# Moving GpSimd combinations, a small matmul and two activations to other places in a two-layer graph-network kernel

One core of one Trainium2 chip. The metric is the device time of one execution, in microseconds (us), as the median of several executions. All executions of this study were in the fast state. Where two kernels are compared by a ratio, it is the mean time of one kernel's fast runs over that of the other's of the same rounds, so it is not quite the ratio of the medians that are quoted beside it. "Slower than after" or "faster than after" by so many us is the difference of two medians. The runs were timed in several rounds, in which the kernel before had medians from 3920.30 to 3922.25 us; a difference of a few us is therefore also read from the traces.

## What is computed

32 graphs of 512 nodes with 512 features, one adjacency matrix for all. Two layers, both with a residual, all in float32:

```python
# layer 0
h = relu(layernorm(x))
q, k, v = h @ Wq + bq, h @ Wk + bk, h @ Wv + bv          # 8 heads of 64
attn = softmax(q @ k.T / 8 + (1 - adj) * -1e9)
x = x + (attn @ v) @ Wo + bo
# layer 1
h = relu(layernorm(x))
g = h @ W                                                # 512 x 512
e = leaky_relu(g @ a1 [:, None] + g @ a2 [None, :], 0.2) * adj
x = x + elu(softmax(e) @ g + beta * g)
```

## The kernel before

The kernel works on three graphs at once. In step b of its loop, layer 0 of graph b (V and four head pairs) runs beside the last projection (Wo) of graph b-1, layer 1 of graph b-2, and the transposes, K and Q of graph b+1. Every projection (V, K, Q, Wo) is done in blocks with seven products instead of eight; a product is 16 matmuls and takes TensorE 1.73 us. The right-hand blocks of these products are differences of blocks, "combinations", which GpSimd makes: three in `combos`, the fourth in `fourth`.

```python
def combos(b, name, pairs):                 # three GpSimd operations
    ...
    nc.gpsimd.tensor_tensor(t3, b22, b12, op=ALU.subtract)
    nc.gpsimd.tensor_tensor(b12, b12, b11, op=ALU.subtract)
    nc.gpsimd.tensor_tensor(t2, b22, b12, op=ALU.subtract)

def turn(b, st):                            # part N: transposes of graph b
    ...
    nc.scalar.activation(h[0], p, AF.Relu)
    st["hT"] = combos(b, "tT", h)           # for V, K and Q of that graph

def values(b, j, st):                       # head pair j, once its exponentials are there
    need("rd"); need("e"); need("es")
    po = st["po"] = psum.tile([P, N], F32, ..., tag="po")
    ...                                     # po = attention times v, 16 matmuls
    pd = st["pd"] = psum.tile([P, N], F32, ..., tag="pd")
    ...                                     # pd = column sums of the exponentials, 4 matmuls

def finish(b, j, st):                       # reciprocal of pd on VectorE, then o * rd on GpSimd
    for k in range(2):
        later("rd", 0.0, GAP[(j + 1) % NP] - 4.0, 1.7, lambda k=k: divide(k))

def unit(b, j):
    values(...)                             # of the pair before
    for k, tag in enumerate(("s", "xy", "qz", "s")):
        scores(b, j, k, s, tag)             # four score products of this pair
    finish(...)                             # of the pair before

order = {
    0: "0V1N2c3wKQ", 1: "0VU1r2NRW3KQ", B - 1: "0VDU1G2rYRW3", B: "0DUGrRWY", B + 1: "DGY",
}.get(b, "0VDU1G2rYNRW3KQ")
```

The string at the end is the order of the parts in a step: digits are the units of head pairs; D, G and Y are layer 1 (row sums `pe` and diagonal, the gather `pg`, the product `py`); U makes Wo's combinations; r and R add the residual; W is Wo. `later`, `then` and `need` do not run anything on the chip. They decide at build time, with a small model of the clock, where in VectorE's, ScalarE's and GpSimd's instruction streams an operation is written: `later` puts it where the model sees room, `need` writes at once all that is outstanding of a kind. GpSimd took its operations in the written order here: where the change below writes the three combinations behind Wo's own, GpSimd's timeline has them behind too (L348 at 2575.07 us after L356 at 2571.37; before, L348 at 1047.24 ahead of L356 at 1054.50). The names in the profile: `y_w`, `qz_w` are accumulators of Wo's products, `_k` of K's; `ps` scores, `po` attention output, `pd` denominators, `pe` layer 1's row sums. A bank is one accumulator of TensorE's output memory; `pd` has one, so a new pd waits until VectorE has read the last one (29 waits of up to 2.0 us for the reciprocals `rd` in the kernel before).

Of the kernel before, what the change touches and what calls it, by code (L numbers as in the profile page):

```python
# [20 lines left out]
P = 128  # L21
# [40 lines left out]
def kernel(  # L62
# [122 lines left out]
        now = max(clock["dve"], clock["pe"])  # L185
        spare.append((key, now + wait, cost, fn, now + by))

    def then(key, fn):

        ends.append((key, clock["dve"], fn))  # L190

    def need(key):

# [164 lines left out]
    def turn(b, st):  # L358

        xs = st["x"]  # L360
        need(("x", b))
        h = [pair(b, "hT", i, "hP", 2) for i in range(2)]

        def turned(p, c):
            for t in range(T):
                nc.tensor.transpose(p[:, ts(t, P)], xs[t][:, ts(c, P)], ident)

        for c, tag in ((2, "po"), (3, "qz")):
            p = psum.tile([P, 1 if c == 2 else 2, N], F32, name=f"pn{c}_{b}", tag=tag)[:, 0, :]
            turned(p, c)  # L370
            nc.scalar.activation(h[1][:, c - 2, :], p, AF.Relu)
        p = psum.tile([P, 2, N], F32, name=f"pn0_{b}", tag="s")
        for c in range(2):
            turned(p[:, c, :], c)
        nc.scalar.activation(h[0], p, AF.Relu)
        pe(2.4)
        st["hT"] = combos(b, "tT", h)

    def seven(name, w, B, tokens, one, two, scale=1.0, more=None):

# [147 lines left out]

    def values(b, j, st):

        need("rd")
        need("e")
        need("es")
        po = st["po"] = psum.tile([P, N], F32, name=f"po_{b}_{j}", tag="po")
        e, v = st["e"][j], st["v"]
        for k in range(T):
            for s in range(2):
                nc.tensor.matmul(  # L538
                    po[s * HD : (s + 1) * HD, :],
                    v[k // 2][:, k % 2, (2 * j + s) * HD : (2 * j + s + 1) * HD],  # L540
                    e[k][:, s, :], start=k == 0, stop=k == T - 1,
                )
        pd = st["pd"] = psum.tile([P, N], F32, name=f"pd_{b}_{j}", tag="pd")
        for s in range(2):
            nc.tensor.matmul(  # L545
                pd[s * HD : (s + 1) * HD, :], ones[:, :HD], st["es"][j][:, s, :], start=True, stop=True
            )
        pe(4.5)
        if j % 2 == 0:
            st["o"].append(pair(b, "oT", j // 2, "oP", 3))  # L550
        nc.scalar.copy(st["o"][j // 2][:, j % 2, :], po)  # L551

    def finish(b, j, st):

        o = st["o"][j // 2][:, j % 2, :]
        rd = wtile([P, N], f"rd_{b}_{j}", "rd", 1)

        def divide(k):
            nc.vector.reciprocal(rd[:, ts(k, H)], st["pd"][:, ts(k, H)])  # L559
            if k:  # L560
                then("rd", rest)

        def rest():
            junk = wtile([P, N], f"rj_{b}_{j}", "rj", 1, BF16)
            nc.scalar.activation(junk, rd, AF.Copy, accum_out=rsum[:, b, j : j + 1])  # L565
            nc.gpsimd.tensor_tensor(o, o, rd, op=ALU.mult)  # L566

        for k in range(2):
            later("rd", 0.0, GAP[(j + 1) % NP] - 4.0, 1.7, lambda k=k: divide(k))

    def residual(b, st, i, tag="x1", bufs=3):

# [34 lines left out]
    def norm1(b, st, rows):  # L607

        key = ("hn", b)

        mv = st["mv"][:, rows[0] : rows[-1] + 1, :]
        rstd = wtile([P, 2], f"rs1_{b}_{rows[0]}", "rs1", 2)

        def first(i):
            t = rows[i]
            stats(st["x1"][t // 2][:, t % 2, :], f"b{b}_{t}", mv[:, i, :])
            if i:
                root(rstd, mv)
                later(key, 2.5, 6.0, 0.4, second)

        def second():
            nb = wtile([P, 2], f"nb_{b}_{rows[0]}", "nb", 2)
            nc.vector.scalar_tensor_tensor(nb, mv[:, :, 0], -1.0, rstd, op0=ALU.mult, op1=ALU.mult)

            def rest():
                for i, t in enumerate(rows):
                    hn = wtile([P, D], f"hn_{b}_{t}", "hn", 4)
                    nc.scalar.activation(  # L628
                        hn, st["x1"][t // 2][:, t % 2, :], AF.Relu,
                        bias=nb[:, i : i + 1], scale=rstd[:, i : i + 1],  # L630
                    )
                    st["hn"][t] = hn
                    for g, r in ((0, wa1_r), (1, wa2_r)):
                        later(key, 1.2 + i, 10.0, 0.8, lambda t=t, g=g, r=r: third(t, g, r))

            then(key, rest)

        def third(t, g, r):
            scr = wtile([P, D], f"scr_{b}_{t}_{g}", "y", 3)
            nc.vector.tensor_tensor_reduce(  # L640
                scr, st["hn"][t], r, 1.0, 0.0, op0=ALU.mult, op1=ALU.add,
                accum_out=st["s12"][:, g, t : t + 1],
            )
            st["dots"] += 1
            if st["dots"] == 2 * T:
                logits(b, st)

        for i in range(2):
            later(key, 0.0, 6.0, 0.95, lambda i=i: first(i))

    def logits(b, st):

        s12 = st["s12"]
        row = wtile([P, N], f"s1_{b}", "s1", 1)
        as_row(row, s12[:, 0, :], f"s1_{b}", mix=True)

        def start(k):
            z = wtile([P, N], f"at_{b}_{k}", "at", 4)
            nc.vector.scalar_tensor_tensor(
                z, row, s12[:, 1, k : k + 1], adjT[:, k, :], op0=ALU.add, op1=ALU.mult  # L660
            )
            nc.vector.scalar_tensor_tensor(z, z, ALPHA, z, op0=ALU.mult, op1=ALU.max)  # L662
            st["at"].append(z)

            def rest():
                nc.scalar.activation(z, z, AF.Exp)  # L666
                if k:
                    later(("at", b), 1.0, 8.0, 0.75, total)

            def total():  # L670
                if k == 1:
                    st["as"] = wtile([P, N], f"as_{b}", "as", 1)
                nc.vector.tensor_tensor(st["as"], st["at"][0] if k == 1 else st["as"], z, op=ALU.add)

            then(("at", b), rest)

        for k in range(T):
            later(("at", b), 4.5, 20.0, 1.5, lambda k=k: start(k))
# [75 lines left out]
    def step(b):  # L754



        cur, nxt = states.get(b), states.get(b + 1)
        prev, old = states.get(b - 1), states.get(b - 2)

        def run(pieces):
            for _ in pieces:
                pass

        def V():
            run(proj_v(b, cur))

        def G():
            for c in range(C):
                gather(b - 2, c, old)  # L770

        def Y():
            for t in range(T):
                final(b - 2, t, old)

        def turned():
            turn(b + 1, nxt)
            if b + 2 < B:
                new_state(b + 2)

        def W():
            need("wa")
            fourth(b - 1, "uT", prev["oT"])
            run(out_proj(b - 1, prev))

        def K():
            fourth(b + 1, "tT", nxt["hT"])
            run(proj_k(b + 1, nxt))

        def U():  # L790
            need("rd")
            prev["oT"] = combos(b - 1, "uT", prev["o"])

        parts = {
            "V": V, "D": lambda: diagonal(b - 2, old), "G": G, "Y": Y, "N": turned, "W": W,
            "K": K, "U": U, "r": lambda: residual(b - 1, prev, 0, *(("e", 4) if b == B else ())),
            "R": lambda: residual(b - 1, prev, 1, *(("e", 4) if b == B else ())),
            "Q": lambda: run(proj_q(b + 1, nxt)),
            "c": lambda: value_row(ao, bvr), "w": row_constants,
        }  # L800
        order = {
            0: "0V1N2c3wKQ", 1: "0VU1r2NRW3KQ", B - 1: "0VDU1G2rYRW3", B: "0DUGrRWY", B + 1: "DGY",
        }.get(b, "0VDU1G2rYNRW3KQ")
        for part in order:
            if part.isdigit():
                unit(b, int(part))
            else:
                parts[part]()
        if b == 0:
            need("nm")  # L810
            need("bad")
        if b == B + 1:
            judge()
        states.pop(b - 2, None)
# [18 lines left out]
    with tc.manual_schedule(engines=BY_HAND):  # L833
# [7 lines left out]

        y_ = psum.tile([P, N], F32, name="y_first", tag="y")
        qz = psum.tile([P, 2, N], F32, name="qz_first", tag="qz")
        for _ in range(6):
            for p in (y_, qz[:, 0, :], qz[:, 1, :]):
                for t in range(T):
                    product(nc, p[:, ts(t, P)], ones, ident, start=t == 0, stop=t == T - 1)
        need(("x", 0))
        combine(nc.vector, wk, ak)
        turn(0, states[0])  # L850
        fourth(0, "tT", states[0]["hT"])
        edges()
        combine(nc.gpsimd, wq, aq)
# [221 lines left out]
```

## Time and profile before

| | before |
|---|---|
| time, median of 3 runs | 3922.25 us (3919.39 to 3922.41) |
| span of the profiled run | 3920.0 us |
| TensorE busy | 3657.1 us, 93% |
| one steady step, mean of 28 | 117.98 us, some 116.99 and some 118.69 |
| mean granted TensorE clock | 0.978 |

The steady step is read from TensorE's timeline, from one gather to the next. TensorE is nearly full, so the table says where to look: not for work but for holes in TensorE's stream that come once a step. The prediction shows those lines and reads them.

### The profile page before, as it was taken

The numbers are of one execution on the slowest core, as the hardware profiler recorded it, in microseconds if no ns is written. First come the engines' busy times: TensorE is split into PE (matmuls) and PEld (weight loads), VectorE is DVE, ScalarE is ACT, GpSimd is POOL, SyncE is SP. The second block draws the span as 40 slices with busy tenths as digits, with TensorE's granted clock in tenths as the row PEclk, the third lists the DMA queues.
The fourth block names the chain that finished last, engine by engine and source line by source line (L and its number), as shares of the span: only waits on it lengthen the run. The fifth ranks groups of instructions, "written<-read, shape, count | busy, mean of one in ns | idle before, by whom it ended". The sixth has DMA issues, their size and how long they took to land.

```text
span 3920.0 us, 58754 instructions
## 1 busy us (share of the span) xinstructions
PE 3657.1 (93%) x24402; PEld 1800.4 (46%) x24402; DVE 2765.8 (71%) x4121; ACT 1399.4 (36%) x2086; POOL 1197.2 (31%) x960
## 2 busy tenths in 40 slices
PE   8889999999999999999999999999999999999976
PEld 5344444454444454444444444444444444444422
DVE  6666777776777767777776777776777776777753
ACT  3323333333433333333333333333333333343321
POOL 4223332223332323332333322333322333322331
PEclk9889999999999999999999999999999999999988
DMA  4001010111110111010111010111110111010000
GB/s 122 9 14 36 33 36 6 33 36 36 33 36 4 36 36 36 33 36 4 36 36 36 33 36 4 36 36 36 33 36 3 36 36 36 33 33 7 25 30 25
DMA packets 71728, 120.83 MB, mean 31 GB/s; under 512 B 12384, under 2 KB 16480, under 8 KB 71456
## 3 DMA queue, kind: packets, MB, share of 16 engines
q1 hardware_dynamic: 70160, 115.70, 9.6%
q8 instruction: 193, 3.16, 0.3%
q10 hardware_dynamic: 1088, 1.05, 0.1%
q14 instruction: 79, 0.65, 0.1%
q0 software_dynamic: 208, 0.27, 0.0%
HBM read 83.37 MB, written 33.63 MB: 30 GB/s over the span
## 4 chain that ended last, share of the span: by engine, by line
PE 72%; DVE 11%; POOL 9%; ACT 5%; issue 3%; DMA 0%; ACTq 0%; POOLq 0%; DVEq 0%; SPq 0%
PE pg L51 11%; PE py L51 11%; PE ps L497 10%; PE po L538 8%; PE qz_v L51 4%; PE qz_q L51 4%; PE qz_k L51 3%; PE pd L545 3%; PE x_v L51 3%; DVE rd L559 3%; PE x_q L51 3%; PE y_v L51 3%; PE y_q L51 3%; DVE e L507 2%; PE qz_w L51 2%
## 5 line engine op out<-in xcount | busy, mean ns | idle before, releaser
L566 POOL TENSOR_TENSOR oT<-oT,rd 128x512 f32<-128x512 f32 x128 | 190.5, 1488 | 1755.4 <-DVE rd L559 1711.3
L520 ACT ACTIVATE e<-e 128x1024 f32<-128x1024 f32 x512 | 540.8, 1056 | 343.5 <-DVE e L507 309.5
L507 DVE TENSOR_TENSOR e<-ps,nmT 128x1024 f32<-128x1024 f32 x384 | 457.1, 1218 | 254.6 <-PE ps L497 254.6
L538 PE MATMUL po<-e,v 128*64 128x512 f32 x2048 | 479.2, 610 | 11.7 <-ACT e L520 11.5
L497 PE MATMUL ps<-qT,kT 64*128 64x512 f32 x2048 | 484.8, 613 | 5.5 <-DVE e L507 5.5
L51 PE MATMUL pg<-at,hn 128*64 128x512 f32 x2048 | 450.8, 598 | 4.2 <-DVE dmax L699 2.1
L51 PE MATMUL py<-w,gT 128*64 128x512 f32 x2048 | 446.4, 594 | 0.0
L559 DVE RECIPROCAL rd<-pd 128x256 f32<-128x256 f32 x256 | 434.3, 1729 | 0.0
L729 POOL TENSOR_TENSOR y<-y,x 128x512 f32<-128x512 f32 x128 | 217.2, 1697 | 559.4 <-DVE y L727 445.1
L517 DVE TENSOR_TENSOR es<-es,e 128x1024 f32<-128x1024 f32 x256 | 345.8, 1351 | 9.0 <-ACT e L520 0.7
L497 PEld LDWEIGHTS ps<-qT,kT 64*128 64x128 f32 x2048 | 190.3, 190 | 299.9 <-issue 204.0
L51 PEld LDWEIGHTS pg<-at,hn 128*64 128x64 f32 x2048 | 146.0, 138 | 303.9 <-issue 279.5
L51 PEld LDWEIGHTS py<-w,gT 128*64 128x64 f32 x2048 | 145.1, 137 | 296.9 <-issue 273.4
L538 PEld LDWEIGHTS po<-e,v 128*64 128x64 f32 x2048 | 149.7, 143 | 275.0 <-issue 247.8
L551 ACT COPY oT<-po 128x512 f32<-128x512 f32 x128 | 73.8, 577 | 506.7 <-PE po L538 506.7
L51 PE MATMUL qz_w<-wo,uT 128*64 128x256 f32 x1024 | 135.1, 410 | 80.3 <-DVE x L587 80.2
L545 PE MATMUL pd<-es,ones 128*64 128x512 f32 x512 | 137.3, 615 | 74.7 <-DVE rd L559 57.4
L640 DVE CUSTOM_DVE_ANT_0 scr<-hn,wa_r 128x512 f32<-128x512 f32 x256 | 164.0, 687 | 59.6 <-ACT hn L628 59.6
L725 ACT ACTIVATE y<-py,rd 128x512 f32<-128x512 f32 x128 | 88.0, 687 | 284.7 <-PE py L51 284.7
L666 ACT ACTIVATE at<-at 128x512 f32<-128x512 f32 x128 | 80.7, 631 | 275.5 <-DVE at L662 275.5
L565 ACT ACTIVATE rj<-rd 128x512 bf16<-128x512 f32 x128 | 80.7, 630 | 255.2 <-DVE rd L559 255.1
L712 ACT COPY gT<-pg 128x512 f32<-128x512 f32 x128 | 75.1, 587 | 268.9 <-PE pg L51 268.9
(179 smaller groups left out, 5705.2 us busy)
## 6 DMA issues: line engine op xcount, KB each, us to landing
x<-in_x_dram SPq DMA_DIRECT2D x128, 256.0 KB, 3.0
x<-in_x_dram SPq DMA_DIRECT2D x64, 512.0 KB, 4.5
out_dram<-y SPq DMA_DIRECT2D x128, 256.0 KB, 2.2
s<-row_s SPq DMA_DIRECT2D x32, 256.0 KB, 3.6
adj<-in_adj_dram SPq DMA_DIRECT2D x4, 256.0 KB, 7.4
w<-in_L_gnn_W_dram SPq DMA_DIRECT2D x1, 1024.0 KB, 7.9
wk<-in_L_gnn_Wk_dram ACTq DMA_DIRECT2D x3, 256.0 KB, 5.0
wq<-in_L_gnn_Wq_dram SPq DMA_DIRECT2D x3, 256.0 KB, 5.5
```

What stands on the lines that cost most here:

```text
L51: nc.tensor.matmul(out[s : s + HD], lhsT[:, s : s + HD], rhs, start=start, stop=stop, skip_group_check=onto)
L497: nc.tensor.matmul(ps[s], st["kT"][j][rows, ts(k, P)], st["qT"][j][rows, :], start=True, stop=True)
L507: nc.vector.tensor_tensor(e, p, nmT[:, k, :].unsqueeze(1).to_broadcast([P, 2, N]), op=ALU.add)
L517: nc.vector.tensor_tensor(es, one, e, op=ALU.add)
L520: nc.scalar.activation(e, e, AF.Exp)
L538: nc.tensor.matmul(po[s * HD : (s + 1) * HD, :], v[k // 2][:, k % 2, (2 * j + s) * HD : (2 * j + s + 1) * HD], e[k][:, s, :], start=k == 0 ...
L545: nc.tensor.matmul(pd[s * HD : (s + 1) * HD, :], ones[:, :HD], st["es"][j][:, s, :], start=True, stop=True)
L559: nc.vector.reciprocal(rd[:, ts(k, H)], st["pd"][:, ts(k, H)])
L566: nc.gpsimd.tensor_tensor(o, o, rd, op=ALU.mult)
L640: nc.vector.tensor_tensor_reduce(scr, st["hn"][t], r, 1.0, 0.0, op0=ALU.mult, op1=ALU.add, accum_out=st["s12"][:, g, t : t + 1],)
L725: nc.scalar.activation(y, p, AF.Exp, scale=r)
L729: nc.gpsimd.tensor_tensor(y, y, st["x1"][t // 2][:, t % 2, :], op=ALU.add)
```

## The change

Its intent is to close the holes. `combos` of the next graph move from the transposes to a part of its own, H, behind Wo. The product pd moves from `values` to `finish`, that is behind the next scores, so that it waits less for VectorE to have read the one bank of pd. The relus of layer 1 no longer come in pairs. Step 1 moves Wo forward; step 32 puts Wo of the last graph first; two of six warm-up rounds go. For the last graph, two kinds of layer 1's tiles borrow other buffers, which is left out here. Cut to its core:

```diff
-        st["hT"] = combos(b, "tT", h)
+        st["h"] = h
...
     def values(b, j, st):
-        need("rd")
...
-        pd = st["pd"] = psum.tile([P, N], F32, name=f"pd_{b}_{j}", tag="pd")
-        (four matmuls into pd)
     def finish(b, j, st):
+        need("rd")
+        pd = psum.tile([P, N], F32, name=f"pd_{b}_{j}", tag="pd")
+        (four matmuls into pd)
...
-            later("rd", 0.0, GAP[(j + 1) % NP] - 4.0, 1.7, lambda k=k: divide(k))
+            later("rd", 0.0, GAP[(j + 1) % NP] + 3.0, 1.7, lambda k=k: divide(k))
...
-            def rest():                      # both relus of a pair of row blocks at once
+            def rest(i):                     # one relu
...
-            then(key, rest)
+            for i in range(2):
+                then(key, lambda i=i: rest(i), 1.8 * i)
...
+        def H_():
+            nxt["hT"] = combos(b + 1, "tT", nxt["h"])
...
-            0: "0V1N2c3wKQ", 1: "0VU1r2NRW3KQ", B - 1: "0VDU1G2rYRW3", B: "0DUGrRWY", B + 1: "DGY",
-        }.get(b, "0VDU1G2rYNRW3KQ")
+            0: "0V1N2c3HwKQ", 1: "0VUrR1W2NH3KQ", B - 1: "0VDU1G2rYRW3", B: "0UrRWDGY", B + 1: "DGY",
+        }.get(b, "0VDU1G2rYNRWH3KQ")
...
-        for _ in range(6):
+        for _ in range(4):
```

More of the change, by code (lines that the diff above doesn't have):

```diff
@@ L186, in later, with then @@
         spare.append((key, now + wait, cost, fn, now + by))
-    def then(key, fn):
-        ends.append((key, clock["dve"], fn))
+    def then(key, fn, wait=0.0):
+        ends.append((key, clock["dve"] + wait, fn))
     def need(key):
@@ L542, in values, with finish @@
                 )
-        pd = st["pd"] = psum.tile([P, N], F32, name=f"pd_{b}_{j}", tag="pd")
+        pe(3.5)
+        if j % 2 == 0:
+            st["o"].append(pair(b, "oT", j // 2, "oP", 3))
+        nc.scalar.copy(st["o"][j // 2][:, j % 2, :], po)
+    def finish(b, j, st):
+        need("rd")
+        pd = psum.tile([P, N], F32, name=f"pd_{b}_{j}", tag="pd")
         for s in range(2):
@@ L547, in values @@
             )
-        pe(4.5)
-        if j % 2 == 0:
-            st["o"].append(pair(b, "oT", j // 2, "oP", 3))
-        nc.scalar.copy(st["o"][j // 2][:, j % 2, :], po)
-    def finish(b, j, st):
+        pe(0.95)
         o = st["o"][j // 2][:, j % 2, :]
@@ L558, in divide @@
         def divide(k):
-            nc.vector.reciprocal(rd[:, ts(k, H)], st["pd"][:, ts(k, H)])
+            nc.vector.reciprocal(rd[:, ts(k, H)], pd[:, ts(k, H)])
             if k:
@@ L623, in second @@
             nc.vector.scalar_tensor_tensor(nb, mv[:, :, 0], -1.0, rstd, op0=ALU.mult, op1=ALU.mult)
-            def rest():
-                for i, t in enumerate(rows):
-                    hn = wtile([P, D], f"hn_{b}_{t}", "hn", 4)
-                    nc.scalar.activation(
-                        hn, st["x1"][t // 2][:, t % 2, :], AF.Relu,
-                        bias=nb[:, i : i + 1], scale=rstd[:, i : i + 1],
-                    )
-                    st["hn"][t] = hn
-                    for g, r in ((0, wa1_r), (1, wa2_r)):
-                        later(key, 1.2 + i, 10.0, 0.8, lambda t=t, g=g, r=r: third(t, g, r))
-            then(key, rest)
+            def rest(i):
+                t = rows[i]
+                hn = wtile([P, D], f"hn_{b}_{t}", "hn" if b < B - 1 else "x", 4)
+                nc.scalar.activation(
+                    hn, st["x1"][t // 2][:, t % 2, :], AF.Relu,
+                    bias=nb[:, i : i + 1], scale=rstd[:, i : i + 1],
+                )
+                st["hn"][t] = hn
+                for g, r in ((0, wa1_r), (1, wa2_r)):
+                    later(key, 1.2, 10.0, 0.8, lambda t=t, g=g, r=r: third(t, g, r))
+            for i in range(2):
+                then(key, lambda i=i: rest(i), 1.8 * i)
         def third(t, g, r):
@@ L657, in start @@
         def start(k):
-            z = wtile([P, N], f"at_{b}_{k}", "at", 4)
+            z = wtile([P, N], f"at_{b}_{k}", "at" if b < B - 1 else "qT", 4)
             nc.vector.scalar_tensor_tensor(
@@ L795, in step @@
             "V": V, "D": lambda: diagonal(b - 2, old), "G": G, "Y": Y, "N": turned, "W": W,
-            "K": K, "U": U, "r": lambda: residual(b - 1, prev, 0, *(("e", 4) if b == B else ())),
+            "K": K, "U": U, "H": H_, "r": lambda: residual(b - 1, prev, 0, *(("e", 4) if b == B else ())),
             "R": lambda: residual(b - 1, prev, 1, *(("e", 4) if b == B else ())),
@@ L850 @@
         turn(0, states[0])
+        states[0]["hT"] = combos(0, "tT", states[0]["h"])
         fourth(0, "tT", states[0]["hT"])
```

## The prediction

> **What bounds the kernel now.** I read the page's busy table first, then what TensorE waited for, then the order of time in one step of the loop over the 32 graphs, then GpSimd and VectorE beside it.

> ```profile
> PE 3657.1 (93%) x24402; PEld 1800.4 (46%) x24402; DVE 2765.8 (71%) x4121; ACT 1399.4 (36%) x2086; POOL 1197.2 (31%) x960
> ...
> PE qz_w L51 <- DVE x L587: 80.2, 29, 3.2
> PE pd L545 <- DVE rd L559: 57.4, 29, 2.0
> PE pe L51 <- DVE as L673: 48.3, 3, 24.5
> PE pd L545 <- DVE es L517: 17.3, 6, 6.1
> PE qz_k L51 <- ACT qz_k L412: 14.0, 29, 0.5
> ```

> The first line is the busy table: TensorE works 93% of the 3920 us span, so its 263 us of idle time are all that a reordering can win; no matmul is removed. The others are the waits (total us, times, longest). Three of them come 29 times: once per step of the steady loop. They are the target.

> Where they sit, in TensorE's timeline (start, length, idle before):

> ```profile
> 1054.28 1.90 PE L51 MATMUL y_w<-wo,oT 128*64 128x256 f32 x16
> 1058.99 1.95 PE L51 MATMUL qz_w<-wo,uT 128*64 128x256 f32 x16 [2.81 <-DVE x L587]
> ...
> 1114.77 3.61 PE L538 MATMUL po<-e,v 128*64 128x512 f32 x16
> 1120.36 1.08 PE L545 MATMUL pd<-es,ones 128*64 128x512 f32 x4 [1.98 <-DVE rd L559]
> ...
> 1175.98 2.83 PE L51 MATMUL qz_w<-wo,uT 128*64 128x256 f32 x16 [2.81 <-DVE x L587]
> 1178.59 4.46 PE L538 MATMUL po<-e,v 128*64 128x512 f32 x16
> ```

> From start to start, the last of the seven Wo products comes 4.71 us after the one before, where undisturbed ones come every 1.73: 2.98 lost. pd starts 5.59 us after po, undisturbed 3.43: 2.16 lost. The small K wait costs 0.65 (2.38 against 1.73). Together 5.79 us. The last pair of lines shows a second price: in that step the same products take 2.83 and 4.46 us, not 1.95 and 3.60. In 15 of the 29 steps about 1.7 us go this way. Steps are therefore 116.99 or 118.69 us; from the gather at 417.94 to that at 3721.27, 28 steps, the mean is 117.98.

> [...] the slow 1.7 us only follow the 2.81 us stall (or the pd stall, where 16 score matmuls took 5.40 for 3.70), in some steps and not in others; the 0.48 us stalls never have them. So removing the stall should remove them too. [...] GpSimd's y adds take 2.18 us beside VectorE's es sums and 1.27 otherwise.

> **Part 1: hT's combinations behind Wo.** GpSimd works in program order:

> ```profile
> 1047.24 1.28 POOL L348 TENSOR_TENSOR tT<-hT,hT 128x512 f32<-128x512 f32 x1
> 1048.60 2.14 POOL L349 TENSOR_TENSOR hT<-hT 128x512 f32<-128x512 f32 x1
> 1050.81 1.27 POOL L350 TENSOR_TENSOR tT<-hT,hT 128x512 f32<-128x512 f32 x1
> 1052.04 2.50 POOL L576 TENSOR_TENSOR x<-x,c_row 128x512 f32<-128x512 f32 x2
> 1054.50 1.27 POOL L356 TENSOR_TENSOR uT<-uT,oT 128x512 f32<-128x512 f32 x1
> 1055.73 1.26 POOL L566 TENSOR_TENSOR oT<-oT,rd 128x512 f32<-128x512 f32 x1
> 1056.95 2.48 POOL L603 TENSOR_TENSOR x<-x,q_w 128x512 f32<-128x512 f32 x2
> ```

> The stalled product overwrites a bank that VectorE must read first (L587), and that read needs L603's first half, 1058.2. The three combinations cost 4.8 us ahead of it. Without them: residual 1047.24 to 1049.74, fourth combination to 1051.0, oT to 1052.3, first half of L603 to 1053.5. VectorE can read once the product before ends, about 1054.5, and is done at 1055.2; the stalled product is due at 1056.0. The wait goes, with 0.8 us to spare. The residual's load was issued at 1041.99 and needs 4.5 us, so it has landed by 1047.24. The combinations now run while TensorE does po, scores and pd (8.0 us) before K; K's second product comes 9.8 us after Wo, and they need 4 to 5. **Gain 2.98**, and the half-rate time, 15 x 1.7 over 28 steps: **0.9**.

> **Part 2: pd behind the next scores.** pd waited because VectorE still had to read the last pd: after D's small operations it started the two reciprocals at 1116.93 and ended at 1120.30. In the built order of the new kernel this place is unchanged, but the scores take pd's old place at 1118.2. Their first product's sum (L507) has to wait behind the reciprocals: 1120.30 to about 1121.5. The fourth score product uses the bank of the first and is due 2.66 us after the start, at 1120.9, so it waits about 0.7. **The wait of 2.16 becomes one of about 0.75.** At the other three places of a step the built order puts the reciprocals before the next scores or beside K and Q, and I find no wait.

> **Part 3: relus spread.** ScalarE's bank copy for K (L412) stood behind four relus of 0.73 us. Now it is interleaved, but the new order puts y_k's copy behind the last exponential and one relu: ready about 11.6 us after Wo's end, due at 11.5. **0.65 becomes about 0.2.** The sums of layer 1's row end just before D's product is due (about 20.0 against 20.1 after Q's end); I allow 0.1.

> A steady step then: 110.9 us of products (seven x 1.73 for V, W, K, Q; four each of 3.43, 0.96 and 3.64; 13.8 + 13.9 + 1.9 + 0.9) plus 0.75 + 0.2 + 0.1, and 0.3 for what I overlooked: **112.2 against 117.98, 5.8 a step**. Over 28 steps: 162 us; step 2, which has less to lose, 6; step 31's pd wait with its half-rate time, 4.

> **Part 4: start.** Two warm-up rounds of 2.62 us go. VectorE has the normalised x at 14.0, the warm-up ran to 19.6: **5 us** gained. The first steps are mixed. In steps 0 and 1 the built order puts reciprocals behind the next scores' sums, and pd has one bank, so pd will wait some 4 to 6 us in about four places (five score additions take 4.7 us, two reciprocals 3.4, against scores of 3.6 from which pd is due). Against that, waits of 4.4, 3.6, 2.3, 4.0 and 6.1 us for exponentials and sums go. Wo of graph 0 moving forward should bring about 10. Together I count **13 us** gained, with an error of 8.

> **Part 5: end.** The old end waits 16.84 and 24.54 us for layer 1's sums of graphs 30 and 31:

> ```profile
> 3806.76 1.22 PE L51 MATMUL pe<-ones,as 128*64 128x64 f32 x16 [16.84 <-DVE as L673]
> 3877.01 1.23 PE L51 MATMUL pe<-ones,as 128*64 128x64 f32 x16 [24.54 <-DVE as L673]
> ```

> The change puts Wo of 31 before D of 30, and G and Y of 30 before D of 31: meant to hide both. The built order says otherwise. VectorE now has the normalisation scales of graph 30 (nb) behind the first residual addition of Wo 31, which comes after that product's stalls: pd of head pair 3 waits for the reciprocals of pair 2 (to about 16 us after Wo of 30 ends), reciprocals, division and combinations follow to about 25, fourth combination and L603 to 35. Dots of graph 30 then end at about 42; the row's round trip through DRAM took 5.0 us, logits and sums 7.8: D of 30 at 55, where before it was at 37 but with Wo (12.1) still to come. G and Y follow (3.3, 15.5, 13.8). The normalisation of 31 stands behind Y's third group, so its chain of some 22.5 us still hangs at the end: D of 31 at 110.5, before 107.25. **A loss of 3 us**, not a gain of 40.

> Sum: 162 + 6 + 4 + 13 - 3 = 182 off 3922 is 3740. Hand-made schedules mostly miss waits, not invent them, so I put the point at **3747 us**.

> **Rivals.** (a) GpSimd remains late: L603 or the residual's load still holds the last Wo product. For it: the load is issued behind other traffic on one queue. Against it: its issue at 1041.99. If half the wait stays, about 1.5 x 29 = 43 us and the half-rate time 25 come back: 3810. (b) The pd wait only moves: scores waiting behind the reciprocals for the full 2 us, and half-rate time with it. That is 1.4 a step more, 40 us: 3787. (c) VectorE becomes the bound around V, where layer 1's logits have slid later and end within 0.1 us of D's product. Half a microsecond or one there costs 15 to 30 us: 3775. (d) The end works as meant: 16.8 + 24.5 less Wo's own stalls, 20 to 30 us better: 3720.

> **Range and chances.** (b) and (c) are each some 15% likely, (a) 10%, (d) 10%. Eight times in ten between 3722 and 3785. Two per cent faster means below 3844, which needs only 78 of the 182: 0.96; within 2% 0.035; slower 0.005.

> **What would show it.** Right: TensorE busy rises to 97% of the span, its waits lack the qz_w group and the pd group of 29, and a new group of 29 waits of the score product for L507, 0.5 to 1 us each, appears; steps of 112 to 113 us, all of one length; two long waits for layer 1's sums remain at the end. Wrong: a group of 29 that I don't name, over 1 us each; steps that still alternate by 1.7; or an end with no long wait.

## The result

| | before | after |
|---|---|---|
| time, median of 4 runs each, same rounds | 3921.94 us (3919.39 to 3922.41) | 3743.94 us (3742.24 to 3746.36) |
| ratio of the fast runs, 95% interval | | 0.9548 (0.9531 to 0.9564) |
| span of the profiled run | 3920.0 us | 3741.4 us |
| granted clock | 0.978 | 0.986 |

The busy table's first line and the largest waits of TensorE (total us, times, longest us) in the kernel after; line numbers differ by up to seven from those before:

```profile
PE 3618.7 (97%) x24306; PEld 1879.3 (50%) x24306; DVE 2787.5 (75%) x4121; ACT 1400.3 (37%) x2086; POOL 1127.7 (30%) x960
...
PE pe L51 <- DVE as L675: 47.7, 4, 22.9
PE pd L552 <- DVE rd L560: 29.5, 6, 5.6
PE ps L497 <- DVE e L507: 11.1, 31, 2.7
```

The groups of 29 waits for `qz_w`, `pd` and `qz_k` are gone. One new group of about one wait a step has come, the scores `ps` behind L507, but each is small (0.28 us in the step below). Two waits of about 20 us for layer 1's sums (`pe`) stand as before, and pd waits in six places outside the steady loop.

The place where Wo's last product stalled, on TensorE and on GpSimd (start, length):

```profile
2575.06 1.90 PE L51 MATMUL y_w<-wo,oT 128*64 128x256 f32 x16
2576.79 1.90 PE L51 MATMUL qz_w<-wo,uT 128*64 128x256 f32 x16
```
```profile
2572.61 2.50 POOL L604 TENSOR_TENSOR x<-x,q_w 128x512 f32<-128x512 f32 x2
2575.07 1.27 POOL L348 TENSOR_TENSOR tT<-hT,hT 128x512 f32<-128x512 f32 x1
```

The products now follow each other by 1.73 us. L604's first half ends at about 2573.86, 2.9 us before the last product starts; hT's combinations (L348 and on) stand behind it.

The place of the pd stall, VectorE and TensorE:

```profile
2522.38 3.36 DVE L560 RECIPROCAL rd<-pd 128x256 f32<-128x256 f32 x2
2525.65 1.16 DVE L507 TENSOR_TENSOR e<-ps,nmT 128x1024 f32<-128x1024 f32 x1
```
```profile
2523.75 2.85 PE L497 MATMUL ps<-qT,kT 64*128 64x512 f32 x12
2526.87 1.13 PE L497 MATMUL ps<-qT,kT 64*128 64x512 f32 x4 [0.28 <-DVE e L507]
2527.93 1.08 PE L552 MATMUL pd<-es,ones 128*64 128x512 f32 x4
```

The reciprocals are as late as before, but now three score products run beside them. The fourth waits for L507; it starts 3.12 us after the first where 2.66 is undisturbed, so 0.46 us are lost instead of 2.16.

Where the 178.6 us between the two profiled spans lie (from TensorE's two timelines):

| stretch | predicted gain | measured gain |
|---|---|---|
| 28 steady steps, mean 117.98 to 112.07 us (median after 112.05) | 162 | 165.4 |
| start, up to the first gather (298.76 to 284.93) | 13 | 13.8 |
| step 2 | 6 | 4.7 |
| step 31, from the last steady gather to the end of Wo of graph 30 | 4 | 0.3 |
| end of Wo of graph 30 to D of graph 31 (107.25 to 113.1) | -3 | -5.9 |
| the rest | 0 | 0.2 |

### The profile page after: what moved, and what is told of

Its sections match the earlier page's. It is cut to its first block, busy times and chain, and to the rows that moved or that the text cites. A ratio compares the mean times of both kernels' runs of the same rounds, so it can differ in the third digit from the quotient of the medians.

```text
span 3741.4 us, 58868 instructions
## 1 busy us (share of the span) xinstructions
PE 3618.7 (97%) x24306; PEld 1879.3 (50%) x24306; DVE 2787.5 (75%) x4121; ACT 1400.3 (37%) x2086; POOL 1127.7 (30%) x960
## 4 chain that ended last, share of the span: by engine, by line
PE 89%; DVE 9%; issue 1%; DMA 0%; ACT 0%; POOL 0%; DVEq 0%; ACTq 0%; POOLq 0%; SPq 0%
PE pg L51 12%; PE py L51 12%; PE ps L497 10%; PE po L537 9%; PE qz_k L51 4%; PE qz_v L51 4%; PE qz_w L51 4%; PE qz_q L51 4%; PE pd L552 3%; DVE rd L560 3%; PE y_k L51 3%; PE x_v L51 3%; PE x_k L51 3%; PE y_v L51 3%; PE x_q L51 3%; PE x_w L51 3%
## 5 line engine op out<-in xcount | busy, mean ns | idle before, releaser
L567 POOL TENSOR_TENSOR oT<-oT,rd 128x512 f32<-128x512 f32 x128 | 165.7, 1295 | 1590.9 <-DVE rd L560 1588.3
L507 DVE TENSOR_TENSOR e<-ps,nmT 128x1024 f32<-128x1024 f32 x384 | 455.2, 1213 | 104.4 <-PE ps L497 104.4
L537 PE MATMUL po<-e,v 128*64 128x512 f32 x2048 | 465.0, 594 | 0.0
L51 PE MATMUL pg<-at,hn 128*64 128x512 f32 x2048 | 448.8, 596 | 4.2 <-DVE dmax L702 4.2
L51 PE MATMUL py<-w,gT 128*64 128x512 f32 x2048 | 444.9, 592 | 0.0
L731 POOL TENSOR_TENSOR y<-y,x 128x512 f32<-128x512 f32 x128 | 190.8, 1490 | 572.6 <-DVE y L729 513.6
L517 DVE TENSOR_TENSOR es<-es,e 128x1024 f32<-128x1024 f32 x256 | 317.5, 1240 | 20.6 <-ACT e L520 8.0
L51 PEld LDWEIGHTS pg<-at,hn 128*64 128x64 f32 x2048 | 148.8, 138 | 297.8 <-issue 296.9
L51 PEld LDWEIGHTS py<-w,gT 128*64 128x64 f32 x2048 | 147.8, 137 | 291.7 <-issue 291.1
L537 PEld LDWEIGHTS po<-e,v 128*64 128x64 f32 x2048 | 158.4, 138 | 236.2 <-issue 226.9
L545 ACT COPY oT<-po 128x512 f32<-128x512 f32 x128 | 73.9, 577 | 412.2 <-PE po L537 412.2
L566 ACT ACTIVATE rj<-rd 128x512 bf16<-128x512 f32 x128 | 80.8, 631 | 326.1 <-DVE rd L560 326.0
L642 DVE CUSTOM_DVE_ANT_0 scr<-hn,wa_r 128x512 f32<-128x512 f32 x256 | 162.2, 689 | 49.1 <-ACT hn L629 49.1
L517 DVE TENSOR_TENSOR es<-e,e 128x1024 f32<-128x1024 f32 x128 | 183.1, 1431 | 4.3 <-PE pd L552 4.3
L728 DVE TENSOR_SCALAR y<-y 128x512 f32<-128x512 f32 x128 | 55.0, 430 | 167.8 <-ACT y L727 167.8
L306 POOL TENSOR_TENSOR rs<-rs,mhalf 128x2 f32<-128x2 f32 (+1 forms) x96 | 78.4, 816 | 326.3 <-DVE rs L305 312.2
```

The costliest lines, as they stand in the source:

```text
L51: nc.tensor.matmul(out[s : s + HD], lhsT[:, s : s + HD], rhs, start=start, stop=stop, skip_group_check=onto)
L507: nc.vector.tensor_tensor(e, p, nmT[:, k, :].unsqueeze(1).to_broadcast([P, 2, N]), op=ALU.add)
L517: nc.vector.tensor_tensor(es, one, e, op=ALU.add)
L537: nc.tensor.matmul(po[s * HD : (s + 1) * HD, :], v[k // 2][:, k % 2, (2 * j + s) * HD : (2 * j + s + 1) * HD], e[k][:, s, :], start=k == 0 ...
L567: nc.gpsimd.tensor_tensor(o, o, rd, op=ALU.mult)
L642: nc.vector.tensor_tensor_reduce(scr, st["hn"][t], r, 1.0, 0.0, op0=ALU.mult, op1=ALU.add, accum_out=st["s12"][:, g, t : t + 1],)
```

## The experiments

Theory T: TensorE's stream is the bound; each per-step stall before is a late predecessor on another engine (GpSimd's order for Wo, VectorE's for pd, ScalarE's for K), and each part of the change takes one of them away. Its rivals are that one part does it all, that the waits only move, or that the slow products of some steps have a cause of their own. "Slow products" are those that take longer than the same products elsewhere, at worst about twice as long (3.63 us for 1.95 in a timeline below). The recorded texts say "half rate": the clock granted in these places reads 0.50 (1176.89 to 1180.30 us in the kernel before). "Slow time" is the excess of TensorE's groups over the median of the same group, summed over those clearly above it (by over 6%), from 340 to 3480 us: before 24.2 us, after 0.

### Each part undone alone

**u_combos**: the kernel after, with hT's combinations ahead of the residual and of Wo again.

```diff
-        }.get(b, "0VDU1G2rYNRWH3KQ")
+        }.get(b, "0VDU1G2rYNHRW3KQ")
```

> The new kernel with one part undone: hT's combinations again ahead of the residual and of Wo on GpSimd. If GpSimd's queue is what held the last Wo product, the wait of that product for the residual addition returns, 28 or 29 times. Its size by the new order (oT's division now stands ahead of Y's last addition): Y's addition ends about 4.4 us after the transposes start, combinations to 8.5, residual to 11.0, fourth combination to 12.2, first half of L604 to 13.5, addition to 14.2, product due at 12.3: 1.9 us, so 2.1 a step and about 60 us: 3804 us, without half-rate time or with little of it. Rival (the combinations' place is not what counts; the pd or the spread relus bring the gain): within 10 us of 3744.

Measured 3812.57 us (3810.86 to 3813.15), ratio to before 0.9723 (0.9708 to 0.9738): 68.6 us slower than after. TensorE's largest wait:

```profile
PE qz_w L51 <- DVE x L588: 51.8, 30, 2.1
```

The named wait is back, and nothing else. Its length is 1.6 us in 14 and some 2.0 us in another 14 of the 28 steady steps (113.8 and 114.15 us); slow products follow 7 of the longer ones and none of the shorter, and make those steps 115.84 us (slow time 11.5 us).

**u_pd**: pd back in `values`, ahead of the scores, with its `need("rd")` and the earlier reciprocals.

```diff
     def values(b, j, st):
+        need("rd")
...
+        pd = st["pd"] = psum.tile(...)      # and its four matmuls, no longer in finish
-            later("rd", 0.0, GAP[(j + 1) % NP] + 3.0, 1.7, ...)
+            later("rd", 0.0, GAP[(j + 1) % NP] - 4.0, 1.7, ...)
```

> The new kernel with pd put back before the next scores, and the reciprocals' deadline with it. Theory: the pd wait of 1.98 us (2.16 with restart) returns 28 times and the score product's wait of 0.27 (0.4) goes: about 1.75 a step, 50 us; the start's five pd waits for reciprocals (24.6 us) give way to waits for sums of about the same. 3790 us; up to 3815 if half-rate time comes with the stall. Rival (scores behind the reciprocals cost as much as pd did): within 10 us of 3744.

Measured 3837.81 us (3835.69 to 3839.88), ratio 0.9787 (0.9772 to 0.9802): 93.9 us slower than after, and beyond what I had expected. Two places of TensorE's timeline, one step apart:

```profile
1093.43 1.08 PE L545 MATMUL pd<-es,ones 128*64 128x512 f32 x4 [1.99 <-DVE rd L560]
1094.43 3.70 PE L497 MATMUL ps<-qT,kT 64*128 64x512 f32 x16
...
1207.26 1.19 PE L545 MATMUL pd<-es,ones 128*64 128x512 f32 x4 [1.98 <-DVE rd L560]
1208.39 5.24 PE L497 MATMUL ps<-qT,kT 64*128 64x512 f32 x16
```

The same stall is followed by scores of 3.70 us here and of 5.24 there. Steps without slow products are 113.84 us, 1.79 longer than after, as expected. But in 18 of the 26 steps between 440 and 3480 us the scores are slow; slow time is 31.0 us. Of the 93.9 us, 28 x 1.79 = 50.1 are the stall, about 31 the slow time, and 9.4 lie in step 2 (123.85 us against 114.45), which I had not foreseen.

**u_relu**: both relus of a pair at once again.

```diff
-            for i in range(2):
-                then(key, lambda i=i: rest(i), 1.8 * i)
+            then(key, rest)                 # rest loops over both row blocks
```

> The new kernel with the four relus of layer 1 given in pairs again. Theory: K's product waits 0.48 us (0.65 with restart) for ScalarE's bank copy in every step again: 19 us, 3763 us. Rival: once the combinations are away and the scores are earlier, the relus end before the copy is due and nothing changes: 3744 us.

Measured 3763.61 us (3762.96 to 3766.61), ratio 0.9601 (0.9588 to 0.9614): 19.7 us slower than after, as expected. TensorE's new wait:

```profile
PE y_k L51 <- ACT y_k L401: 23.7, 29, 0.8
```

It is K's other copy, `y_k`, not the `qz_k` copy of the kernel before: with hT's combinations moved, the relus stand in front of another instruction. No slow products followed these stalls of up to 0.8 us (slow time 0).

**u_end**: the old order of step 32.

```diff
-            B: "0UrRWDGY"
+            B: "0DUGrRWY"
```

> The new kernel with the old order of step 32 (D of graph 30 and its gather ahead of Wo of 31). By the two traces the new end is 5.9 us longer from Wo of 30 to D of 31, so this should be 3738 us, 0.15% faster. Rival, the intent of the change: the new order hides waits of 16.8 and 24.5 us, then the old one costs 20 to 40 us: 3765 to 3785.

Measured 3737.28 us (3736.47 to 3739.07), ratio 0.9532 (0.9519 to 0.9545): 6.7 us faster than after. The change's new end loses a little, as the prediction said, and does not gain the two long waits; the rival (the new order hides them), 20 to 40 us the other way, falls. The 95% intervals of the two ratios overlap (0.9519 to 0.9545 and 0.9531 to 0.9564), so the loss is shown by the traces, 5.9 us, more than by the ratios.

The three undone parts of the loop cost 68.6, 93.9 and 19.7 us. That they add up to 182 us, about the whole gain, is partly chance: two of them contain slow time that came with the undoing (11.5 and 31.0 us, where before had 24.2 once), and the start's 13.8 us are in none. The slow time is not a term of one part, which the next runs show.

### What the slow products are

**b_combos**: the kernel before with part 1 alone, the combinations behind Wo.

```diff
-        st["hT"] = combos(b, "tT", h)
+        st["h"] = h                         # and combos(b + 1, ...) as part H, behind W
-        }.get(b, "0VDU1G2rYNRW3KQ")
+        }.get(b, "0VDU1G2rYNRWH3KQ")
```

> The kernel before with part 1 alone: hT's combinations behind Wo, all else as it was. Theory: 2.98 us a step go, 29 x 2.98 = 86, to 3834 if the half-rate time stays the same size (now brought on by the pd stall of 1.98 us, in two steps of three, as in the kernel after with only the pd part undone, where it was 31 us: 3842), 3810 if it goes with the stall. Rival (parts 1 and 2 only work together, the wait for GpSimd being replaced by another): over 3880.

Measured 3848.12 us (3846.40 to 3850.39), ratio 0.981 (0.9794 to 0.9827): 73.7 us less than before, not the 86 of the stall. Part 1 works alone, and the wait for `qz_w` is gone. But slow time rose from 24.2 to 34.7 us: it now follows the pd stall, in 22 of 28 steps.

**b_fill**: the kernel before, with 32 unneeded products into a free bank in Wo's stall.

```diff
+        if tokens and more:                 # Wo only, ahead of its last product
+            junk = psum.tile([P, 2, N], F32, name=f"junk_{name}", tag="s")
+            for h in range(2):
+                for t in range(T):
+                    product(nc, junk[:, h, ts(t, P)], ones, ident, start=t == 0, stop=t == T - 1)
         times(z_, NA22, "t4", False, onto=True)
```

> The kernel before, with 32 unneeded products (about 1.74 us) put into the stall of 2.81 us ahead of Wo's last product, into a free bank. It gives TensorE more work and takes no wait away: the last product still starts when VectorE has read its bank. Theory (the slow 1.7 us are TensorE's half rate, brought on by the idle stretch): the stall shrinks to about 1.1 us of idle time and the slow products after it vanish, some 15 x 1.7 = 25 us, so 3896 us, though the kernel does more. Rival (the slow products come from something else, such as traffic to the memories at that place): 3921, as before.

Measured 3927.68 us (3925.97 to 3929.73, 20 runs), ratio 1.0015 (1.0008 to 1.0022): 5.9 us slower than before. Neither number came. TensorE's timeline says why:

```profile
1060.40 1.95 PE L51 MATMUL qz_w<-wo,uT 128*64 128x256 f32 x16 [1.08 <-DVE x L593]
1062.18 3.60 PE L544 MATMUL po<-e,v 128*64 128x512 f32 x16
...
1121.77 1.36 PE L551 MATMUL pd<-es,ones 128*64 128x512 f32 x4 [1.98 <-DVE rd L565]
1123.06 5.07 PE L503 MATMUL ps<-qT,kT 64*128 64x512 f32 x16
```

Where the idle time was cut to 1.08 us, the products after it are quick, in all 26 steps looked at: at this place the slow time did come with the idle time. But it turned up behind the other stall of the step, pd's 1.98 us, in 14 of 25 steps, where the kernel before had it twice in the whole run (at 530 and 3715 us). The sum (24.9 us) is that of before. One stall cured was not enough here, with a second of 1.98 us left.

**pd_fill**: u_pd, with the same 32 products in its only long stall.

```diff
     (u_pd, in values, ahead of pd)
+        if j == 0 and 1 < b < B - 1:
+            junk = psum.tile([P, 2, N], F32, name=f"junk_{b}", tag="s")
+            (32 products into junk, as in b_fill)
```

> The kernel after with the pd part undone (3837.8 us, a stall of 1.98 us a step ahead of pd), and now 32 unneeded products of about 1.74 us in that stall. Theory (half rate follows an idle stretch of about 2 us): the stall becomes 0.3 us, the slow products go, about 30 us: 3807, steps of 113.9 all of one length. Rival: 3838 and steps that differ by 1.7.

Measured 3802.37 us (3800.79 to 3806.27), ratio 0.9699 (0.9682 to 0.9715): 35.4 us faster than u_pd by adding work. TensorE:

```profile
1080.37 1.08 PE L550 MATMUL pd<-es,ones 128*64 128x512 f32 x4 [0.24 <-DVE rd L565]
1081.38 3.70 PE L497 MATMUL ps<-qT,kT 64*128 64x512 f32 x16
```

The steady steps are 113.84 us, slow time 0. Only the last differs: the edit leaves it unfilled, it still has a stall of 1.99 us, its scores are slow again, and it takes 115.49 us. The place of pd and VectorE's lateness are those of u_pd; the idleness is gone (0.24 us for 1.99), and the slow time with it (0 for 31.0 us). This settles that the slow products of u_pd followed from TensorE being idle.

**d_pool**: the kernel after, with three more GpSimd operations ahead of the fourth combination for Wo. They multiply a constant row by ones.

```diff
+            cr = c_row.rearrange("p (a q) -> p a q", q=P)
+            for _ in range(3):
+                nc.gpsimd.tensor_tensor(cr, cr, ones.unsqueeze(1).to_broadcast([P, T, P]), op=ALU.mult)
             fourth(b - 1, "uT", prev["oT"])
```

> The kernel after with three more GpSimd operations of 1.27 us each (they multiply a constant row by ones, so the result stays) ahead of the fourth combination for Wo. In the trace of the kernel after, the first half of the scaled addition ends at 2573.86, VectorE's addition of 0.69 then waits for the product until 2575.45 and ends at 2576.1, and the last product starts on time at 2576.79: GpSimd has 2.2 us to spare, so three operations (3.8 us) should bring a wait of 1.6 us in every step: 3744 + 29 x 1.6 = 3790, and up to 30 more if 1.6 us are enough to bring the half rate. If GpSimd's lateness is not what held Wo's last product (rival): 3744.

Measured 3836.46 us (3835.11 to 3840.25), ratio 0.9785 (0.9769 to 0.9802): 92.5 us slower than after; I had 46 to 76. GpSimd's lateness is what holds Wo's last product, and the spare time of some 2 us was read rightly: the wait is 1.75 us in 13 of 27 steps (the operations took 4.0 us, not 3.8). The other 14 have 2.10 or more:

```profile
1837.88 3.63 PE L51 MATMUL qz_w<-wo,uT 128*64 128x256 f32 x16 [2.11 <-DVE x L588]
...
2644.23 1.95 PE L51 MATMUL qz_w<-wo,uT 128*64 128x256 f32 x16 [1.76 <-DVE x L588]
```

None of the 13 stalls of 1.75 us is followed by slow products; 13 of the 14 of 2.1 us are, all in one run of steps from 793 to 2186 us. The slow steps are 116.06 us, the others 114.03. Of the 92.5 us, 55.4 come from the longer basic step (28 x 1.98: the stall of 1.75 and 0.23 more) and 26 from the 13 slow steps of 2.03; the rest lies outside the 28 steps. GpSimd's timeline shows why the stall has two lengths: in the 14 steps of 2.1 us the multiplication by pd's reciprocal (L567, 1.27 us) stands between the fourth combination and L604, in the 13 of 1.75 us it comes ahead of Y's last addition.

```profile
1054.01:1057.42 3.41, 2.17 (x22) 1.00 0.02 7
1057.42:1060.84 3.42, 1.85 (x18) 1.00 0.00 0
1060.84:1064.25 3.41, 3.41 (x20) 1.00 0.00 0
...
1173.48:1176.89 3.41, 0.91 (x8) 1.00 0.00 0
1176.89:1180.30 3.41, 3.41 (x14) 0.50 0.00 0
```

In the quick step the grid cuts the same stall in two, 1.24 and 1.57 us of idle time. In the slow step 2.50 us fall into one stretch, and the next one runs at half clock, which costs 1.7 us. Over the six runs (5343 stretches) half clock followed 82 of the 86 stretches with 1.9 us of idle time or more, 4 of the 10 with 1.8 to 1.9, and none of the 5247 with less. In these runs, then, stalls of 1.08 and 1.75 us brought no half clock wherever they fell, those of 1.98 us only where over 1.8 us of idle time fell into one stretch, and the one of 2.81 us that the grid cuts at 1057.42 brought none. By stall, slow products came after 1.08 us of idle time (once 1.49) in 0 of 26 steps (b_fill), after 1.75 us in 0 of 13 and after 2.10 us or more in 13 of 14 (d_pool), after 1.98 us in 18 of 26 (u_pd), after 2.81 us in 14 of 28 (before).

The slow steps also lie close to whole grid lengths. Those of d_pool (116.06 us) come to 34.0 lengths of 3.413 us, and 13 of them came in a row, their half-clock stretches 34 lengths apart; two steps of before (116.99 + 118.69) are 69.05, and 10 of the 13 distances between its half-clock stretches from 440 to 3480 us are 235.52 us, 69.0 lengths; three steps of u_pd (115.49 + 115.53 + 113.84) are 101.03. That this sets the share of slow steps is an estimate: no run shifted the loop against the grid to test it.

### The end and the start

**n_end**: the kernel after, made to write the normalisation and dots of graph 30 ahead of the last Wo, those of graph 31 ahead of the gather of 30, and the logits of 31 ahead of Y of 30.

```diff
+            "h": lambda: need(("hn", b - 2)), "k": lambda: need(("hn", b - 1)),
+            "a": lambda: need(("at", b - 1)), "b": lambda: need(("at", b - 2)),
...
-            B: "0UrRWDGY"
+            B: "0hUrRWDkGaY"
```

> The kernel after with the program made to give VectorE and ScalarE the normalisation of graph 30 (the relus and dots of layer 1) before the last Wo, that of graph 31 before the gather of 30, and the logits of 31 before the matmul of Y of 30. In the kernel after the first stands behind the residual additions of the last Wo (normalisation scales at 3620.20, D of 30 at 3642.43 after a wait of 17.88 us), the second behind Y's third group (D of 31 at 3698.61 after 22.86). Theory (the order of VectorE's instructions, not the amount of work, makes both waits): the chain of some 22.5 us of graph 31 lies beside G and Y, 30 us, so D of 31 follows Y at once, -22.9; D of 30 waits some 10 us less: about 3714. Rival (VectorE and the row's way through DRAM are too long whatever the order): over 3735.

In the kernel after, graph 30's scales were written behind a residual addition of the last Wo, and D of the two last graphs stood idle for 17.88 and 22.86 us:

```profile
3620.20 1.47 DVE L624 SCALAR_TENSOR_TENSOR nb<-mv,rs 128x2 f32<-128x2 f32 x2
```
```profile
3642.43 1.22 PE L51 MATMUL pe<-ones,as 128*64 128x64 f32 x16 [17.88 <-DVE as L675]
...
3698.61 1.22 PE L51 MATMUL pe<-ones,as 128*64 128x64 f32 x16 [22.86 <-DVE as L675]
```

Measured 3720.63 us (3718.39 to 3723.30), ratio 0.9493 (0.9480 to 0.9506): 23.3 us faster than after. In n_end the same two places:

```profile
3637.04 1.22 PE L51 MATMUL pe<-ones,as 128*64 128x64 f32 x16 [8.63 <-DVE as L675]
...
3670.64 1.06 PE L51 MATMUL pe<-ones,as 128*64 128x64 f32 x16
```

The second wait is gone, the first halved. It was VectorE's order and not its load. Less came of it than the 30 us expected; the trace shows one reason: VectorE does the dots of 30 ahead of the reciprocals of the last head pair, so Wo's second product waits 8.95 us for GpSimd instead of 4.89.

**n_end2**: in addition the logits of 30 ahead of the last Wo.

```diff
-            B: "0hUrRWDkGaY"
+            B: "0hUrRbWDkGaY"
```

> As the run before, and the logits of graph 30 are also given ahead of the last Wo. Theory: D of 30 then follows Wo without a wait, 17.9 + 22.9 less what Wo's additions wait for VectorE meanwhile: about 3706. Rival: Wo itself waits for VectorE by what D gains, so the same time as the run before within 3 us.

Measured 3720.67 us (3719.87 to 3721.74), ratio 0.9491 (0.9478 to 0.9504): the same as n_end, so the rival holds. D of 30 follows at once, but Wo pays:

```profile
3628.56 3.68 PE L51 MATMUL y_w<-wo,uT 128*64 128x256 f32 x16 [8.14 <-ACT y_w L401]
```

Wo's bank copy on ScalarE now stands behind the exponentials of these logits, and the logits take up to 1.75 us each (L661, the first 1.70 at 3613.87 us), the first of them beside GpSimd's combinations, for which Wo's second product waits 9.28 us, to 3616.74; n_end has 0.74 (the same instruction at 3629.07 us).

**n_pd**: the kernel after, with the reciprocals of the first two graphs written early, as before.

```diff
-            later("rd", 0.0, GAP[(j + 1) % NP] + 3.0, 1.7, ...)
+            later("rd", 0.0, GAP[(j + 1) % NP] + (3.0 if b > 1 else -4.0), 1.7, ...)
```

> The kernel after with the reciprocals of the first two graphs given early, as the kernel before has them, instead of late. The prediction says that pd waits some 4 to 6 us in about five places of the start because reciprocals stand behind the next scores' sums; the trace of the kernel after has 24.6 us of such waits up to 400 us. Theory: they shrink to the steady loop's 0.3 to 0.8 us each: 3722, and a little more for time at half rate. Rival (VectorE is simply too busy in the start, so that another wait, for the scores' or the exponentials' sums, takes their place): 3735 to 3744.

Measured 3739.65 us (3736.74 to 3741.01), ratio 0.9539 (0.9526 to 0.9552): 4.3 us faster than after. The ratios' intervals overlap (0.9526 to 0.9552 and 0.9531 to 0.9564), but in the trace the first gather comes at 281.1 us, and at 284.9 in after. Of TensorE's waits for pd up to 400 us, one of five went, 24.6 us became 20.4, so the theory that the deadline makes them falls. The rival said that another wait would take their place; that is not what the trace shows either, apart from 1.5 us more for the scores: four of the waits simply stay. The deadline is not what puts those reciprocals late, and what does I have not tested.

**n_best**: the scales and dots of graph 30 behind the last reciprocals instead of ahead of them, and n_pd.

```diff
-            B: "0hUrRWDkGaY"                # n_end
+            B: "0UrRhWDkGaY"                # and the later(...) of n_pd
```

> The run with the normalisations given early (3720.6 us), with that of graph 30 moved behind the reciprocals of the last head pair instead of ahead of them, and the early reciprocals of the first two graphs (-4.3 us in a run of their own). There the dots of 30 (4.9 us) held the reciprocals, so that Wo's second product waited 8.95 us for GpSimd's oT, where the kernel after waits 4.89. Theory: Wo ends 4 us earlier, D of 30 with it since VectorE's logits follow Wo's additions, and all that comes after: 3720.6 - 4 - 4.3 = 3712. Rival: the dots[...] slow GpSimd's combinations beside them, and Wo's second product waits as long as before: 3716. Either would be the fastest of all runs.

Measured 3712.34 us (3712.10 to 3713.56), ratio 0.9472 (0.9459 to 0.9485): the fastest, 31.6 us under the change. Wo's second product waits 5.00 us again. The rival was half right too. The dots on VectorE and GpSimd's residual run side by side, and both lengthen:

```profile
3609.95 6.75 POOL L577 TENSOR_TENSOR x<-x,c_row 128x512 f32<-128x512 f32 x4
```

In n_end the same four operations take 4.95 us (1.24 each, 1.69 here), and a dot takes 0.69 us there and 1.74 here (L642 at 3607.13 us). Wo's last product therefore waits 1.32 us, and of the 4 us hoped for about 2.3 remain in the trace: the gather of graph 31 starts 5.64 us earlier than in n_end, 3.37 of which the start gave.

## Why the prediction was right

Point by point, by its own steps.

**The bound.** TensorE busy rose to 97%, the three groups of 29 waits vanished, and the one group of about 29 that came is the one named, though its waits are 0.28 us and not 0.5 to 1. One sentence was wrong: that the 263 us of idle time are all that can be won, since no matmul is removed. Idle time fell by 140.2 us (262.9 to 122.7), and busy time by another 38.4 (3657.1 to 3618.7): most of it is slow time (24.2 us) and the 96 matmuls of the warm-up.

**Part 1.** The stall of Wo is gone; u_combos brings it back, d_pool brings it back by delaying GpSimd alone, and b_combos shows that it can be had without the other parts. The 0.9 us a step of slow time that the prediction put down to this part is a wrong attribution, and the prediction's "removing the stall should remove them too" is the step that failed. b_combos shows it: with part 1 alone it grew to 34.7 us. It took parts 1 and 2 together: u_pd, with the stall of 1.98 us, has 31.0 us of slow time, and after, with no wait over 0.3 us from 440 to 3480 us, has none. As the change had both, the sum came out right, for this term by luck. (The slow steps before are also 16 of 28, 14 behind Wo's stall and 2 behind pd's, not 15 of 29.)

**Part 2.** "The wait of 2.16 becomes one of about 0.75" is 0.46, because VectorE's score sum starts the moment the reciprocals end and the scores start 0.14 us later than reckoned. u_pd confirms the size without slow time: 1.79 us a step.

**Part 3.** About 0.2 was allowed; K's product `y_k` loses 0.28. Its `qz_k` wait is gone. The 0.1 for D's sums was not needed. u_relu gives 0.70 us a step.

**The steady step.** 112.2 was predicted and 112.07 measured. Of the terms, 0.46 + 0.28 + 0.14 stand where 0.75 + 0.2 + 0.1 was, and about 0.3 remains. The 0.3 that was set aside for the overlooked did cover it, but what it covered is in the sum: the products as printed add up to 111.06 and not 110.9, and the quick steps before, 116.99 less 5.79 of stalls, give 111.2.

**Start.** 13 predicted, 13.8 measured: the predicted pd waits are there, 24.6 us in five places. That they stand behind the next scores' sums is so; that the late deadline puts them there is not (n_pd). The removed warm-up shows as 5.8 us at the first transposes (19.61 to 13.82 us), where 5 were predicted. The move of Wo in step 1 has no run of its own, so its share of the rest, predicted as about 10, stays open.

**Step 31.** 4 predicted, 0.3 measured. This was counted twice: the pd wait of that step lies before the last steady gather, so the 28 steps had it already.

**End.** A loss of 3 predicted, 5.9 measured in the trace and 6.7 by u_end. D of 30 came 56.9 us after Wo of 30, predicted 55; D of 31 came 113.1 after, predicted 110.5. The named mechanism, scales written behind a residual addition, is confirmed by n_end, which moves them and gains 23.3 us.

**The point.** The terms gave 3740, the 7 us that were added for missed waits made it 3747; 3743.94 was measured. The misses partly cancel; in measured gain less predicted gain they are +3.4 us in the steady steps, +0.8 at the start, -1.3 in step 2, -3.7 in step 31 and -2.9 at the end. Rivals (a) to (d) did not come.

## What to carry to other kernels

When one engine is the bound, list its waits that come once per loop step, find for each the engine that was late, and ask what is written ahead of the late instruction that nobody needs yet: moving it was worth the stall here, 2 to 3 us a step. Before crediting a cured stall with more than its own length, look for other stalls of the same kind in the step, since the half-rate time after one moved to the next in b_fill (14 of 25 steps) and b_combos (22 of 28), and lay the granted clock's grid, here 3.413 us, over the stalls. A build-time scheduler's stream must be read as written: one normalisation written a place too late cost some 20 us at the end of this kernel.
